# PSUM as four pairs of banks, scores evicted two heads at a time, key halves added for three units, in a new order

## The chip, the cores and the metric

The kernel runs on one core of one Trainium2 chip. Its metric is the device time of one execution in microseconds. Three runs of the kernel before gave 662.77, 663.51 and 665.59 us; their median is 663.51 us. The profile is one execution with its own time: its instructions span 661.4 us.

## The reference

One block of cross attention with an MLP, in float32. Batch 8, 256 queries and 256 keys, width 512, 16 heads of 32, inner width 2048. Cut to what matters:

```python
x1 = layer_norm(x) * ln1_w + ln1_b
q, k, v = x1 @ q_w + q_b, ctx @ k_w + k_b, ctx @ v_w + v_b      # 16 heads of 32
scores = einsum('bhqd,bhkd->bhqk', q, k) / sqrt(32)             # the mask is all ones
attn = softmax(scores)
out = einsum('bhqk,bhkd->bhqd', attn, v) @ cproj_w + cproj_b
hidden = out + x
y = layer_norm(hidden) * ln2_w + ln2_b
return hidden + gelu(y @ fc_w + fc_b) @ proj_w + proj_b
```

## The kernel before, in words

**Work.** The batch is done in two groups of four (g = 0, 1). The products with weights use two-by-two block schemes with seven products instead of eight (`quad`, line 857). A `quad` named, say, `o0_0` has products P1 to P7 on TensorE into three PSUM buffers X, Y and W, and evictions on DVE or ACT: `t1`, `t2`, `t3` and `c12` out of X after P1, P6, P5 and P3, `c11` out of Y after P2, `c22` and `c21` out of W after P7 and P4. X is written again by the next product only after its eviction. The sums of operands that the scheme needs (for example `a0t1` to `a0t4` of the attention output, `c0t` of the context, `z0i` in the last projection, `kws` of weights) run on DVE or POOL. The MLP (`fc`, `pd`) nests the scheme twice.

**Attention.** A unit `ghb` is group g, four heads (hg) and one batch element b; there are 32. Its steps are:
- `s` (line 1014): eight products of 32 rows on TensorE, four at a time, one head each, scores transposed (keys on partitions). Head j has a PSUM bank of 512 columns: 256 for each half of the 256 keys (kc).
- `ev` (line 1020, by the helper at line 618): ACT adds the mask's column and copies to SBUF, into `pr0` (heads 0, 1) and `pr1` (heads 2, 3). There are eight evictions of 128x256 in a unit, one for each head and key half.
- `mx`, `mt`, `mc`, `fold`: the maximum over keys, by DVE and small ACT copies; `md` and `mm` store it to DRAM and load it back spread over all partitions.
- `less` (line 1042, DVE or POOL) subtracts it, `exp` (line 1054, ACT) follows.
- `av` (line 1061): products with `ones`, which give the sum over the keys, and with v, which give the weighted values, both into one bank. For each head and each key half there is one of either, accumulated over the two halves.
- `r` and `att`: DVE inverts the sums and scales.

There is already a second form: where the letter of the unit in `KINDS` (line 494) is z, the two key halves are added first (`ss`, line 1057, DVE or POOL), and `ones` then takes four products instead of eight (line 1064). Before, all 32 letters are p, and that form is not used.

**Order.** `PROGRAM` (line 124) is one list of every step, written out: each engine's queue is the list's steps of that engine, in the list's order. A letter behind a colon says the engine where there is a choice (V DVE, A ACT, G POOL). All DMAs go on SP. `PLACES` (line 350) gives each buffer its slot. In SBUF the slots are numbered. In PSUM there are eight banks in two families, three W and five C: a scores unit takes any four C banks, and other buffers a bank of either family as `PLACES` says. The framework derives the waits: a buffer's first write waits until everyone is done with the slot's occupant before.

**Names of the prediction's steps.** `turn_c0_al` turns the context of group 0 (four transposes into a bank); `cq` loads it; `vw00` is a quarter of v's weight. `ab`, `a0t`, `o0_*`: bias, sums and output projection of group 0. `stats_y`, `eps`, `pow`, `nb`, `norm_y`, `turn_y`: the second normalisation and its turning. `less110_1` is the subtraction of the maximum in unit 110, heads 2 and 3.

Of the kernel before, what the change touches and what calls it, by code (L numbers as in the profile page):

```python
# [16 lines left out]
P = 128  # L17
# [6 lines left out]
BANKS = {"W": 3, "C": 5}  # L24
# [19 lines left out]
class Order:  # L44
# [49 lines left out]
    def run(self):  # L94
# [30 lines left out]
cq0_00_1 cq0_00_0 vw00 rows1 cq0_01_1 vw11 vw10 cq0_01_0 turn_c0_10 turn_c0_00 kw00 c0_10:V small cq0_11_0 c0_00:A  # L125
cq0_10_1 rows6 v0_0_P1 rows4 cq0_11_1 vws1:G fw0_00_1 turn_c0_11 fw0_11_1 turn_c0_01 vws2:G rows0 c0_11:V v0_1_P1
c0_01:A kw10 v0_0_t1:A fw0_11_0 c0t1:V fw0_00_0 fw0_10_0 v0_1_t1:A cq0_10_0 turn_c0_31 turn_c0_21 c0_31:V k0_1_P1
c0_21:A c0t2:V rows3 fw0i1_1:G k0_0_P1 fw0_10_1 fw0i4_1:G xt0_0 v0_0_P6 rows8 fw0i4_2:V fw0i4_3:G kws3:V vw01 xt0_7
fw0i4_4:G v0_1_P6 kw11 v0_0_t2:V xt0_6 fw0i1_2:V kw01 fw0i1_4:V c0t3:V v0_0_P5 v0_1_t2:A mk fw0s1:V xt0_2 turn_c0_20
vws4:G fw1_01_1 turn_c0_30 stats_x0_00:V c0_20:A xt0_1 v0_1_P5 c0_30:A fw0s3:V xt0_4 fw0i5_1:G v0_0_P2 v0_1_t3:V  # L130
v0_0_t3:A rows7 kws1:G fw0s2:V xt0_3 fw0_01_0 v0_0_P3 fw0i6_1:V rows2 fw0i7_3:G stats_x0_30:V k0_1_P7 fw1_00_1
v0_0_c12:A xt0_5 stats_x0_31:V stats_x0_01:A fw1_00_0 mk~1 fw0i7_1:V fw1_11_1 v0_1_P2 fw0i6_2:V rows5 fw0i6_4:V
fw0i1_3:V fcd0_7_False stats_x0_11:A fw0i6_3:V qw00 vws3:V v0_1_P3 fw1_10_1 eps_x0_0:V stats_x0_10:V fw1_10_0 pow_x0_0
fcd0_4_True nb_x0_0 eps_x0_1:G fw0i7_2:V k0_1_P2 v0_1_c12:A fw0i7_4:G qw10 fw1i1_3:V stats_x0_20:A kws2:G
stats_x0_21:V cols k0_0_P7 fw1_01_0 cols~1 fcd0_5_False pow_x0_1 fw0i5_3:V k0_1_t1:A fw1_11_0 fw0i5_2:V eps_x0_2:G
k0_0_t1:A eps_x0_3:G k0_0_P2 kws4:V norm_x0_01:A pow_x0_3 fw0_01_1 qw11 pow_x0_2 k0_0_P6 k0_0_c11 fcd0_1_True fw1s3:V
xt1_3 k0_1_P6 nb_x0_3 nb_x0_2 fw1i1_1:V norm_x0_21:A k0_0_t2:V fw1i1_2:G norm_x0_31:A nb_x0_1 k0_0_P5 norm_x0_00:V
fw0i5_4:G k0_1_t2:A v0_0_c11 norm_x0_11:A fcd0_5_True fw1i4_1:V fw1i1_4:V fcd0_7_True norm_x0_30:A k0_1_P5 k0_0_t3:V
fcd1_1_True fw1i4_2:G k0_1_c11 fcd0_6_False fw1s1:G fw1i4_4:V k0_0_P3 k0_1_t3:A xt1_2 norm_x0_10:A k0_0_c22 xt1_0
norm_x0_20:A k0_1_P3 v0_1_c11 k0_0_c12:A fw1i4_3:V c0t4:V turn_x0_00 k0_1_c22 turn_x0_10 x0_00:A turn_x0_11 fw0s4:V  # L140
qw01 qws1:G turn_x0_01 x0_10:A fcd0_6_True turn_x0_20 x0_01:A x0_11:V k0_0_P4 xt1_1 fw1i2_1:V fcd1_5_False fcd1_4_True
# [369 lines left out]
def tile_xattn_block(  # L511
# [154 lines left out]
    def col(i):  # L666
        return cols.t[:, i : i + 1]
# [838 lines left out]
```

## Time and profile before

| what | value |
|---|---|
| median of three runs | 663.51 us (662.77 to 665.59) |
| profiled execution: span of its instructions | 661.4 us |
| TensorE matmuls busy | 651.4 us (98%) |
| DVE busy | 571.6 us (86%) |
| ACT busy | 356.5 us (54%) |
| POOL busy | 450.4 us (68%) |
| DMA | 146.94 MB, mean 222 GB/s |
| granted TensorE clock | 1.00 |

The profiled execution's own time is that span; the runs' median lies 2.1 us above it, which holds what is around the first and last instruction and the scatter of runs. A float32 matmul stands as two records in the trace, so a `quad` product of two matmuls has four. Matmuls overlap: the mean of one record (about 380 ns for 256 columns) is longer than the step from one to the next, which the chain of waits shows. A "PE" row is a matmul, "PEld" a weight load. The idle time behind a row's bar is that of the engine ahead of the group's instructions, and the releaser is what ended most of it.

### The profile page before, as it was taken

The page shows a single profiled execution, that of the slowest core. Times are in us where ns is not written, and L with a number is a line of the kernel's source. Part 1 is how long each engine was busy: PE and PEld are TensorE (multiplying, and loading weights), DVE is VectorE, ACT ScalarE, POOL GpSimd, SP SyncE. Part 2 cuts the span into 40 slices and gives each one's busy share as a digit, 9 for nine tenths or more (in the row PEclk, how much of TensorE's full clock was granted, in tenths as well). Part 3 has the DMA queues.
Part 4 walks back from the last instruction along what each step waited for, and adds up shares of the span by engine and source line. Part 5 has one row for each costly group of instructions (what it writes and reads, how often), then busy time and mean ns, then how long its engine had stood idle before and what let it go on. Part 6 is the DMA issues. An engine that isn't in the chain of part 4 may idle for free.

```text
span 661.4 us, 11596 instructions
## 1 busy us (share of the span) xinstructions
PE 651.4 (98%) x3971; PEld 493.3 (75%) x3971; DVE 571.6 (86%) x935; ACT 356.5 (54%) x720; POOL 450.4 (68%) x397
## 2 busy tenths in 40 slices
PE   8999999999999999999999999999999999999997
PEld 6845464477545676787887878888888888888897
DVE  3989799879999999999989989987889779997573
ACT  2365698978989889837688890040222222730000
POOL 2476989868779996988999864659436046314882
PEclk9999999999999999999999999999999999999999
DMA  8999997889888568878555364979999995877256
GB/s 268 323 358 345 228 229 262 287 195 228 236 259 261 174 210 265 270 237 279 163 162 189 129 212 167 304 246 189 192 253 235 247 241 155 179 254 159 49 118 129
DMA packets 216538, 146.94 MB, mean 222 GB/s; under 512 B 125424, under 2 KB 176928, under 8 KB 216480
## 3 DMA queue, kind: packets, MB, share of 16 engines
q1 hardware_dynamic: 216480, 146.21, 78.9%
q8 instruction: 31, 0.51, 0.3%
q14 instruction: 27, 0.22, 0.1%
HBM read 105.67 MB, written 40.50 MB: 221 GB/s over the span
## 4 chain that ended last, share of the span: by engine, by line
PE 52%; DVE 5%; ACT 3%; DMA 1%; issue 1%; POOL 1%; SPq 0%; DVEq 0%
PE fc_X L638 14%; PE pd_X L638 14%; PE pd_W L638 7%; PE fc_W L638 6%; PE pd_Y L638 4%; PE fc_Y L638 3%; PE o_X L638 2%; DVE h L629 1%; PE av L638 1%; ACT pr L1054 1%; PE o_W L638 1%; ACT pr L618 1%; PE s L638 1%; DMA fl<-fcd 1%; DMA qw<-in_L_xattn_cproj_w_dram 1%
## 5 line engine op out<-in xcount | busy, mean ns | idle before, releaser
L618 ACT ACTIVATE pr<-s,cols 128x256 f32<-128x256 f32 x256 | 104.4, 483 | 17.4 <-PE s L638 10.6
L1051 POOL TENSOR_TENSOR pr<-pr,mm 128x512 f32<-128x512 f32 x72 | 98.4, 1393 | 7.7 <-DMA mm<-md 5.2
L1234 ACT ACTIVATE h<-h,cols 128x256 f32<-128x256 f32 x128 | 56.0, 499 | 55.7 <-DVE h L629 54.1
L1024 DVE TRANSPOSE_TENSOR_REDUCE mx<-pr 128x32 f32<-128x1024 f32 x64 | 77.5, 1222 | 2.5 <-ACT pr L618 2.4
L1054 ACT ACTIVATE pr<-pr 128x1024 f32<-128x1024 f32 x64 | 66.6, 1069 | 7.3 <-POOL pr L1051 4.1
L629 DVE TENSOR_TENSOR h<-fc_X,h 128x512 f32<-128x512 f32 x80 | 53.0, 679 | 7.1 <-PE fc_X L638 5.7
L1046 DVE TENSOR_TENSOR pr<-pr,mm 128x1024 f32<-128x1024 f32 x28 | 37.7, 1355 | 0.0
L629 DVE TENSOR_TENSOR h<-fc_W,h 128x512 f32<-128x512 f32 x48 | 32.1, 679 | 5.7 <-PE fc_W L638 5.5
L1033 ACT COPY mx<-mx 32x64 f32<-32x64 f32 x96 | 29.7, 309 | 11.9 <-DVE mx L1030 5.5
L638 PE MATMUL av<-pr,ones 128*32 128x256 f32 x512 | 34.1, 383 | 0.6 <-ACT pr L618 0.5
L610 ACT ACTIVATE e<-pd_X,cols 128x256 f32<-128x256 f32 x7 | 3.3, 471 | 57.0 <-PE pd_X L638 57.0
L629 POOL TENSOR_TENSOR h<-h,fl 128x512 f32<-128x512 f32 x9 | 12.3, 1368 | 25.7 <-DMA out_dram<-tq 22.4
L627 POOL TENSOR_TENSOR z1i<-z1t,z1i 128x512 f32<-128x512 f32 x8 | 10.0, 1270 | 25.5 <-DVE z1i L629 25.5
L638 PEld LDWEIGHTS av<-pr,ones 128*32 128x32 f32 x512 | 14.9, 109 | 16.1 <-issue 5.4
L638 PE MATMUL fc_W<-y1i,fl 128*128 128x256 f32 x100 | 24.5, 380 | 0.0
L638 PE MATMUL fc_X<-y1i,fl 128*128 128x256 f32 x88 | 22.5, 380 | 0.0
L638 PEld LDWEIGHTS fc_W<-y1i,fl 128*128 128x128 f32 x100 | 18.9, 190 | 2.9 <-DVE h L629 0.3
L605 ACT COPY h<-fc_X 128x512 f32<-128x512 f32 x16 | 9.1, 586 | 18.2 <-PE fc_X L638 14.2
L627 POOL TENSOR_TENSOR z1i<-h,z1i 128x512 f32<-128x512 f32 x10 | 13.4, 1362 | 7.8 <-ACT h L1234 4.1
L638 PE MATMUL pd_W<-z0i,pl 128*128 128x256 f32 x80 | 18.6, 379 | 0.0
L638 PEld LDWEIGHTS fc_X<-y1i,fl 128*128 128x128 f32 x88 | 16.7, 190 | 2.5 <-DVE h L629 0.3
L627 POOL TENSOR_TENSOR z0i<-h,z0i 128x512 f32<-128x512 f32 x10 | 16.3, 1653 | 1.4 <-DVE z0i L629 1.2
(601 smaller groups left out, 1905.6 us busy)
## 6 DMA issues: line engine op xcount, KB each, us to landing
mm<-md SPq DMA_DIRECT2D x32, 512.0 KB, 5.1
pl<-prd SPq DMA_DIRECT2D x54, 256.0 KB, 4.4
fl<-fcd SPq DMA_DIRECT2D x40, 256.0 KB, 4.5
fl<-prd SPq DMA_DIRECT2D x23, 256.0 KB, 4.6
fw<-in_L_xattn_fc_w_dram SPq DMA_DIRECT2D x16, 256.0 KB, 5.3
pw<-in_L_xattn_proj_w_dram SPq DMA_DIRECT2D x32, 128.0 KB, 4.2
hid<-in_x_dram SPq DMA_DIRECT2D x8, 512.0 KB, 7.8
hd<-hid SPq DMA_DIRECT2D x8, 512.0 KB, 3.9
```

The source lines that it names most:

```text
L605: (nc.scalar.copy if e == "ACT" else nc.vector.tensor_copy)(to(), of_())
L610: nc.scalar.activation(to(), of_(), AF.Identity, bias=bias(), scale=1.0)
L618: lambda e: nc.scalar.activation(to(), of_(), AF.Identity, bias=bias(), scale=1.0))
L627: nc.gpsimd.tensor_tensor(to()[:, ts(k, 512)], in0()[:, ts(k, 512)], in1()[:, ts(k, 512)], op)
L629: E[e].tensor_tensor(to(), in0(), in1(), op)
L638: nc.tensor.matmul(o(), l(), r(), start=first, stop=True, skip_group_check=True)
L1024: T.op(f"mx{u}_{h}", [("DVE", 1.126)], [(pr[h], None)], [(mx, [h])], lambda e, h=h: nc.vector.tensor_reduce(tile_of(mx)[:, 0:64].rearrange ...
L1033: lambda e, a=a: nc.scalar.copy(turned_()[0:32, 2 * a : 2 * a + 2, :], turned_()[32 * a : 32 * a + 32, 0:2, :]))
L1046: nc.vector.tensor_tensor(p_, p_, m_[:, :, None, :].to_broadcast([P, 2, 2, S]), ALU.subtract)
L1051: E[e].tensor_tensor(p_, p_, at(M, j)[:, None, :].to_broadcast([P, 2, S]), ALU.subtract)
L1054: lambda e, h=h: nc.scalar.activation(tile_of(pr[h]), tile_of(pr[h]), AF.Exp), table="exp")
L1234: lambda e, f=f, b=b, c=c: nc.scalar.activation(at(h[f][b], c), at(h[f][b], c), AF.Gelu_apprx_tanh, bias=col(c_fcb + f * 4 + c), scale=1.0 ...
```

## The change

Four edits in one:

1. PSUM is four tiles of two banks (B0 to B3). A scores unit takes two whole tiles, one for heads 0 and 1 and one for heads 2 and 3. Every other buffer takes half a tile, any of the eight.
2. A scores eviction reads one key half of two heads at once, 512 elements a partition in two runs of 256 out of two banks. A unit has four evictions instead of eight.
3. Three of the 32 units (012, 030 and 103) take the form with the key halves added first. Of their six additions two are on POOL and four on DVE.
4. `PROGRAM` and `PLACES` are new throughout: the order of each engine's queue, the choice of engine, the slots. The list was planned with delays drawn at random. The steps themselves are the same but for those of 2 and 3.

```diff
-BANKS = {"W": 3, "C": 5}
+BANKS = {"W": 8, "C": 8, "S": 4}
...
-                    w = where[b.name]
-                    b.home = w[0] if not w[0].isdigit() else b.kind
-                    b.slot = int(w.lstrip("WC"))
+                    b.slot = int(where[b.name])
...
-KINDS = ("pppppppppppppppp", "pppppppppppppppp")
+KINDS = ("pppppzzppppppppp", "ppppppppppzppppp")
...
-    halves = {}
+    halves, sides = {}, {}
...
+            elif b.kind == "S":
+                b.t = banks.tile([P, 1024], F32, tag=f"B{b.slot // 2}", name=b.name)
+                sides[b.slot // 2] = None
             else:
-                b.t = banks.tile([P, 512], F32, tag=f"{b.home}{b.slot}", name=b.name)
+                s, k = divmod(b.slot, 2)
+                if sides.get(s) is None:
+                    sides[s] = banks.tile([P, 1024], F32, tag=f"B{s}", name=b.name)
+                b.t = sides[s][:, ts(k, 512)]
...
-    first = banks.tile([P, 512], F32, tag="W0", name="first")
+    first = banks.tile([P, 1024], F32, tag="B0", name="first")
...
-        sb = [Buf(f"s{u}_{j}", "C", 2) for j in range(4)]
+        sb = [Buf(f"s{u}_{h}", "S", 4) for h in range(2)]
...
-            (lambda kc=kc, j=j: at(sb[j], kc), lambda kc=kc, j=j: row(k, j)[:, ts(kc, P)], lambda j=j: row(q, j), True)
+            (lambda kc=kc, j=j: at(sb[j // 2], 2 * (j % 2) + kc), lambda kc=kc, j=j: row(k, j)[:, ts(kc, P)], lambda j=j: row(q, j), True)
...
-            for j in range(4):
-                copy(f"ev{u}_{j}{kc}", (pr[j // 2], [2 * (j % 2) + kc]), (sb[j], [kc]), lambda j=j, kc=kc: at(pr[j // 2], 2 * (j % 2) + kc),
-                     lambda j=j, kc=kc: at(sb[j], kc), 256, lambda kc=kc: col(2 * (4 * g + b) + kc))
+            for h in range(2):
+                both = lambda t, kc=kc: t.rearrange("p (i k q) -> p k i q", i=2, k=2)[:, kc]
+                copy(f"ev{u}_{h}{kc}", (pr[h], [kc, 2 + kc]), (sb[h], [kc, 2 + kc]), lambda h=h, both=both: both(tile_of(pr[h])),
+                     lambda h=h, both=both: both(tile_of(sb[h])), 512, lambda kc=kc: col(2 * (4 * g + b) + kc))
```

Of the lists, the parts that the prediction speaks of, TensorE's steps alone. First the start, before and after:

```
before: turn_c0_10 turn_c0_00 small v0_0_P1 turn_c0_11 turn_c0_01 v0_1_P1 turn_c0_31 turn_c0_21 k0_1_P1 k0_0_P1
after:  small turn_c0_01 turn_c0_00 turn_c0_10 turn_c0_11 turn_c0_31 turn_c0_21 v0_1_P1 v0_0_P1 k0_0_P1
```

SP's first loads, before: cq0_00_1 cq0_00_0 vw00 rows1 cq0_01_1 vw11 vw10 cq0_01_0 kw00; after: cq0_00_0 cq0_01_0 cq0_01_1 cq0_00_1 cq0_11_0 cq0_11_1 vw00 vw11 vw10 vw01 kw00. Then the output projection of group 0 and what follows:

```
before: av033 o0_1_P2 o0_0_P2 s110 o0_0_P6 o0_1_P6 s130 o0_0_P5 o0_1_P5 s112 o0_0_P3 o0_0_P7 o0_1_P3 o0_1_P7
        o0_0_P4 o0_1_P4 s132 s101 av100 av110 av102 av122 av120 turn_y0_00
after:  av033 s110 o0_0_P1 o0_1_P1 s120 o0_1_P2 o0_0_P2 s130 o0_0_P6 o0_1_P6 s112 o0_1_P5 o0_0_P5 o0_1_P3 o0_1_P7
        o0_0_P3 o0_0_P7 o0_1_P4 s101 o0_0_P4 s132 av102 av100 av110 av122 turn_y0_00
```

DVE's queue after, around there: o0_0_c22 o0_0_c12 o0_1_c12 o0_1_c21 stats_y0_10 less110_1 o0_0_c21 stats_y0_00 stats_y0_11 stats_y0_20 aggr aggr aggr stats_y0_01 fold112 aggr aggr eps_y0_0 stats_y0_21 aggr nb_y0_1 nb_y0_0.

More of the change, by code (lines that the diff above doesn't have):

```diff
@@ L127 @@
[L127 to L141, printed above, removed]
@@ L212 @@
-ev112_30 o0_0_c22 exp122_0 o0_1_P7 mx112_1 exp102_1 pw1i4_3:G pw1_01_00 o0_0_c12 o0_0_P4 mm120 pw1i4_2:G pw1_10_00
-o0_1_c12 less110_0:G pw1_00_10 mt112 o0_1_c22 mc112_1 pw1_01_10 mc112_3 stats_y0_20 fl001_2 ev130_10 o0_1_P4 mc112_2
-mx130_1 exp102_0 less110_1:G exp122_1 o0_0_c21 s132 fold112 hd0 o0_1_c21 exp110_0 md112 hd3 stats_y0_21 s101 ev132_11
-pw1_00_00 pw1i4_4:G mx130_0 ev132_10 hd1 less120_1:G av100 ev101_00 fl001_0 exp110_1 stats_y0_11 pw1_01_01 stats_y0_01
-ev132_31 aggr_y0_20 ev101_01 aggr_y0_21 stats_y0_00 mm112 ev132_30 av110 stats_y0_10 ev101_31 eps_y0_2:G ev132_00
@@ L347 @@
-so1_12 pd14_P3 pd14_c22 pd14_P4 pd14_c12 st1 pd14_c21 st01
+cq0_00_0 cq0_01_0 cq0_01_1 cq0_00_1 cq0_11_0 cq0_11_1 vw00 vw11 vw10 small turn_c0_01 turn_c0_00 turn_c0_10 turn_c0_11
+turn_c0_31 turn_c0_21 c0_00:A c0_01:A c0_11:A c0_10:V c0t1:V c0_31:A c0_21:V c0t2:V v0_1_P1 v0_0_P1 v0_1_t1:A v0_0_t1:A
+vws1:G vw01 vws2:V vws4:G kw00 cq0_10_0 cq0_10_1 fw0_00_1 fw0_10_0 k0_0_P1 v0_0_P6 turn_c0_30 k0_1_P1 v0_0_t2:A v0_0_P5
+turn_c0_20 c0_20:A v0_1_P6 c0t3:V vws3:V mk fw0_11_1 fw0_11_0 fw0_10_1 fw0_00_0 rows1 rows4 fw1_11_1 kw01 xt0_1 kw10
@@ new lines @@
+xt0_5 rows6 rows2 fw0s1:V c0_30:V fw0s3:V fw0s2:V fw0i1_3:G fw0i4_1:G fw0i5_3:G kws3:G fw0i1_1:G fw0i1_2:G
+stats_x0_01:V v0_1_t2:V mk~1 fw0i7_1:V rows5 kw11 rows3 k0_0_P2 v0_1_P2 v0_0_P2 kws1:V kws2:V fw0i4_3:V v0_0_c11 c0t4:V
+xt0_6 xt0_7 rows8 rows7 rows0 xt0_4 fw0_01_1 xt0_0 fw0_01_0 fw1_10_0 xt0_2 xt0_3 fw1_01_0 fw1_10_1 cols v0_1_P5 cols~1
+v0_0_t3:A stats_x0_31:A stats_x0_30:A stats_x0_00:V eps_x0_3:V fw0i2_1:V k0_1_P2 stats_x0_21:A fw0i1_4:G fw0i5_1:G
+fw0i4_2:G fw0i4_4:G fw1_00_1 fw1_11_0 fcd0_4_True fw1_00_0 k0_1_P7 pow_x0_3 k0_0_t1:V fw0i7_2:G eps_x0_0:G fw0i6_1:G
@@ new lines @@
+mx110_0 mx110_1 mt110 mc102_2 ev120_00 mc110_2 ev120_01 mc102_3 a0t2:V o0_0_t1 fold100 mc110_3 mc102_1 mc110_1 a0t3:G
+a0t4:G ows4:G less122_0:G ows3:G o0_1_P2 o0_0_P2 s130 o0_0_P6 o0_1_t1 fold102 md102 fold110 md110 mm102 md100
+less102_1:G less122_1:V mx120_0 ev130_01 ev130_11 ev130_00 ev130_10 o0_1_P6 s112 o0_0_t2 o0_1_t2 mx120_1 mt120 mx130_0
+o0_1_P5 o0_1_t3 o0_0_P5 ev112_10 mc120_2 ev112_11 exp122_0 mx130_1 mt130 o0_0_t3 o0_0_c11 ev112_00 pw1_00_00 mm100
+pw1_11_10 less100_1:G mm110 fl001_0 pw1_10_11 pw1_00_10 pw1_11_11 less110_0:G less102_0:G o0_1_P3 o0_1_P7 less100_0:V
@@ new lines @@
+exp122_1 mc120_3 mc120_1 exp102_1 exp100_0 ev112_01 exp100_1 o0_1_c11 fold120 o0_1_c22 o0_0_P3 o0_0_P7 mx112_1 mx112_0
+mt112 o0_1_P4 o0_0_c22 o0_0_c12 o0_1_c12 o0_1_c21 stats_y0_10 s101 o0_0_P4 md120 pw1_00_11 mm120 fl001_2 pw1_10_01 hd1
+fl011_2 pw1_00_01 pw1_10_10 hd2 pw1_10_00 fl002_0 less110_1:V o0_0_c21 stats_y0_00 mc112_2 s132 stats_y0_11 stats_y0_20
+aggr_y0_10 aggr_y0_20 aggr_y0_11 stats_y0_01 mc112_1 mc130_3 mc112_3 exp110_0 fold112 aggr_y0_01 aggr_y0_00 ev101_00
+eps_y0_0:V exp102_0 mc130_2 ev101_01 exp110_1 less120_0:G ev132_01 ev132_10 ev132_00 ev132_11 mc130_1 ev101_11
@@ new lines @@
+eps_y0_1:G pow_y0_1 pow_y0_0 less120_1:G stats_y0_21 aggr_y0_21 nb_y0_1 nb_y0_0 av102 av100 av110 av122 norm_y0_00:A
+norm_y0_11:A ev101_10 norm_y0_01:A norm_y0_10:A exp120_0 turn_y0_00 stats_y0_31 mx132_0 y0_00:A exp120_1 turn_y0_10
+turn_y0_20 turn_y0_30 y0_10:A r102 stats_y0_30 fold130 mx132_1 att102 mt132 r122 aggr_y0_31 r100 fl001_3 fl011_1 hd3
+md112 pw1s3:G hd0 fl001_1 mm112 fc001_P1 fc011_P1 pw1i4_1:V eps_y0_2:V aggr_y0_30 y0_20:A mc132_2 fc001_t1:A mc132_1
+fc011_t1:A mc132_3 y0_30:A pw1s1:G y0i1_1:G eps_y0_3:G pow_y0_3 pow_y0_2 pw1i7_3:V y0i1_2:V av120 fc011_P6 fc011_P2
@@ L388 @@
-s100_0=W0 s100_1=W1 s100_2=4 s100_3=1 pr100_0=8 pr100_1=4 mx100=0 mm100=42 s120_0=4 s120_1=2 s120_2=1 s120_3=0
-pr120_0=18 pr120_1=66 mx120=0 mm120=76 s102_0=1 s102_1=4 s102_2=W1 s102_3=2 pr102_0=48 pr102_1=26 mx102=1 mm102=16
-s122_0=W0 s122_1=W1 s122_2=4 s122_3=2 pr122_0=74 pr122_1=2 mx122=2 mm122=14 av100=0 r100=3 rc100=2 att1_00=48 s110_0=0
-s110_1=W1 s110_2=1 s110_3=W2 pr110_0=72 pr110_1=82 mx110=2 mm110=38 av120=1 r120=12 rc120=6 att1_10=46 s130_0=2
-s130_1=0 s130_2=W1 s130_3=1 pr130_0=58 pr130_1=68 mx130=0 mm130=46 av102=3 r102=4 rc102=4 att1_01=88 s112_0=W2
@@ new lines @@
+ps_x0_00=3 x0_00=4 ps_x0_10=1 ps_x0_20=6 x0_10=66 ps_x0_30=2 ps_x0_01=0 x0_01=52 ps_x0_11=7 ps_x0_21=6 x0_11=46
+ps_x0_31=2 c0t1=38 c0t2=54 c0t3=22 c0t4=80 kw00=15 kw01=84 kw10=34 kw11=71 kws1=64 kws2=87 kws3=19 kws4=28 vw00=36
+vw01=63 vw10=8 vw11=72 vws1=37 vws2=45 vws3=20 vws4=29 qw00=21 qw01=44 qw10=46 qw11=85 qws1=12 qws2=52 qws3=42 qws4=65
+x0t1=40 x0t2=26 x0t3=74 x0t4=34 k0_0_X=3 k0_0_11=69 k0_0_Y=1 k0_0_21=68 k0_0_W=5 k0_0_22=76 k0_0_12=31 k0_1_X=6
+k0_1_11=2 k0_1_Y=2 k0_1_21=7 k0_1_W=4 k0_1_22=3 k0_1_12=1 v0_0_X=7 v0_0_11=62 v0_0_Y=2 v0_0_21=33 v0_0_W=5 v0_0_22=57
@@ new lines @@
+s100_1=4 pr100_0=50 pr100_1=18 mx100=1 mm100=78 s120_0=4 s120_1=6 pr120_0=4 pr120_1=6 mx120=2 mm120=78 s102_0=4
+s102_1=0 pr102_0=2 pr102_1=66 mx102=2 mm102=68 s122_0=4 s122_1=2 pr122_0=14 pr122_1=46 mx122=0 mm122=32 av100=2 r100=12
+rc100=9 att1_00=24 s110_0=6 s110_1=4 pr110_0=26 pr110_1=58 mx110=0 mm110=80 av120=4 r120=1 rc120=4 att1_10=46 s130_0=4
+s130_1=6 pr130_0=72 pr130_1=30 mx130=0 mm130=46 av102=3 r102=8 rc102=4 att1_01=26 s112_0=4 s112_1=6 pr112_0=74
+pr112_1=76 mx112=1 mm112=2 av122=1 r122=8 rc122=7 att1_11=78 s132_0=0 s132_1=6 pr132_0=68 pr132_1=84 mx132=2 mm132=8
@@ new lines @@
+av110=0 r110=11 rc110=6 s101_0=2 s101_1=4 pr101_0=48 pr101_1=32 mx101=2 mm101=16 av130=1 r130=6 rc130=4 s121_0=4
+s121_1=6 pr121_0=0 pr121_1=72 mx121=1 mm121=58 av112=3 r112=5 rc112=7 s103_0=6 s103_1=4 pr103_0=62 pr103_1=18 mx103=1
+mm103=68 ss103=66 av132=2 r132=7 rc132=4 s123_0=4 s123_1=6 pr123_0=16 pr123_1=30 mx123=0 mm123=66 av101=2 r101=7
+rc101=9 s111_0=6 s111_1=0 pr111_0=40 pr111_1=8 mx111=2 mm111=68 av121=4 r121=6 rc121=1 s131_0=2 s131_1=6 pr131_0=74
+pr131_1=68 mx131=2 mm131=82 av103=7 r103=2 rc103=9 s113_0=6 s113_1=2 pr113_0=12 pr113_1=66 mx113=0 mm113=80 av123=1
@@ new lines @@
+r123=8 rc123=4 s133_0=6 s133_1=0 pr133_0=40 pr133_1=16 mx133=1 mm133=20 av111=0 r111=4 rc111=2 av131=6 r131=4 rc131=1
+av113=1 r113=7 rc113=8 av133=7 r133=7 rc133=5 a0t1=80 a0t2=76 a0t3=48 a0t4=0 ow00=65 ow01=60 ow10=40 ow11=21 ows1=45
+ows2=11 ows3=56 ows4=88 hid0_0=8 hid0_1=16 hid0_2=22 hid0_3=82 o0_0_X=0 o0_0_Y=3 o0_0_W=7 o0_1_X=1 o0_1_Y=2 o0_1_W=6
+st_y0_0=2 mv_y0_0=7 rs_y0_0=5 xn_y0_00=1 xn_y0_01=19 st_y0_1=9 mv_y0_1=0 rs_y0_1=1 xn_y0_10=59 xn_y0_11=88 st_y0_2=8
+mv_y0_2=3 rs_y0_2=4 xn_y0_20=19 xn_y0_21=7 st_y0_3=6 mv_y0_3=8 rs_y0_3=9 xn_y0_30=12 xn_y0_31=42 ps_y0_00=6 y0_00=50
@@ L459 @@
+rl1=67 rq1_3=70 tq1_3=4 z1i4_1=54 z1i4_2=28 z1i4_3=76 z1i4_4=36 pl14_1=75 pl14_2=63 pl14_6=86 pl14_7=72 pl14_5=16
+pl14_3=53 pl14_4=33 pd14_X=1 ot0=80 pd14_Y=2 pd14_W=6 ot1=30
 """
```

572 lines of the change are left out of this document (267 added, 305 removed).

## The prediction

> **What bounds the kernel now.** I read the page first, then busy time by stage, then TensorE's waits, then the timeline where it waits longest.
>
> ```profile
> span 661.4 us, 11596 instructions
> PE 651.4 (98%) x3971; PEld 493.3 (75%) x3971; DVE 571.6 (86%) x935; ACT 356.5 (54%) x720; POOL 450.4 (68%) x397
> ```
>
> ```profile
> 0.00:20.00 20.00, 17.43 (x104) 13.96 (x105) 7.75 (x10) 4.12 (x6) 6.56 (x14) 1.00 0.88 281
> 180.00:260.00 80.00, 77.34 (x655) 49.58 (x655) 78.27 (x125) 72.31 (x150) 67.25 (x55) 1.00 0.76 239
> 100.00:180.00 80.00, 79.68 (x640) 48.00 (x632) 71.26 (x128) 69.64 (x147) 64.96 (x56) 1.00 0.87 242
> 260.00:380.00 120.00, 119.24 (x814) 93.97 (x813) 112.38 (x190) 91.69 (x181) 110.72 (x100) 1.00 0.63 202
> 380.00:660.00 280.00, 277.72 (x1404) 241.76 (x1402) 229.81 (x365) 67.02 (x131) 144.51 (x115) 1.00 0.80 197
> 640.00:661.40 21.40, 17.94 (x130) 16.91 (x128) 9.25 (x21) 0.00 (x0) 7.38 (x6) 0.98 0.63 120
> ```
>
> The columns are PE, PEld, DVE, ACT, POOL, then granted clock and DMA. TensorE is idle 10.0 us in all (661.4 less 651.4): 2.57 in the first 20 us, 3.46 in the last 21.4 us, and about 4 between. Of those, 0.32 lies in 100:180, 2.66 in 180:260, 0.76 in 260:380. The clock is full. So no order of the work can win much: **the ceiling on what a better order gives in the middle is about 4 us**, plus waits that hide as stretched matmuls. The stretch 180:260 is the one place where another engine is as full as TensorE: VectorE is busy 78.27 of 80 us, ScalarE 72.31.
>
> ```profile
> PE ps_c L725 <- DMA cq<-in_ctx_dram: 1.6, 2, 1.2
> PE o_X L638 <- DVE a0t L629: 1.0, 1, 1.0
> PE first L650 <- DVE warm L645: 1.0, 1, 1.0
> PE s L638 <- DVE q L629: 0.6, 1, 0.6
> PE av L638 <- ACT pr L618: 0.5, 2, 0.4
> PE fc_X L638 <- DVE h L629: 0.4, 2, 0.2
> ```
>
> ```profile
> 222.62 1.38 PE L638 MATMUL s<-vw,xt 32*128 32x256 f32 x16
> 222.75 2.25 DVE L629 TENSOR_TENSOR a0t<-att,a0t 128x1024 f32<-128x1024 f32 x1
> 225.05 2.21 PE L638 MATMUL o_X<-ows,a0t 128*128 128x256 f32 x9 [1.05 <-DVE a0t L629]
> ```
>
> The longest wait of the middle is 1.05 us at 225.05: the output projection waits for the token sum a0t.
>
> **The change part by part.** Prices come from the chain of waits, where TensorE's pieces stand end to end:
>
> ```profile
> 281.14 0.86 PE fc_Y L638 x4
> 285.45 1.86 PE av L638 x32
> 310.10 1.07 PE s L638 x16
> 412.84 1.73 PE pd_X L638 x8
> ```
>
> *Key halves added first (three units, 012, 030, 103).* A unit's av is 32 records in 1.86 us, 0.058 each. The product with ones is half of them, 16; with the halves added it needs 8. Saved: 8 x 0.058 = 0.465 us per unit, three units: **-1.40 us on TensorE**, which is the path. Added are six additions of 128x512, both operands in SBUF: two on POOL, four on DVE. The trace has no such addition of pr; the nearest rows are
>
> ```profile
> L1051 POOL TENSOR_TENSOR pr<-pr,mm 128x512 f32<-128x512 f32 x72 | 98.4, 1393 | 7.7 <-DMA mm<-md 5.2 <-issue 2.4
> L629 DVE TENSOR_TENSOR h<-fc_X,h 128x512 f32<-128x512 f32 x80 | 53.0, 679 | 7.1 <-PE fc_X L638 5.7 <-PE fc_W L638 0.5 <-DMA out_dram<-tq 0.2
> L629 DVE TENSOR_TENSOR h<-h,fl 128x512 f32<-128x512 f32 x5 | 5.3, 1058 | 0.1
> ```
>
> so 1.4 us on POOL and 0.68 to 1.06 on DVE; I take 1.06, the row whose operands also both lie in SBUF. They stand between exp and av. In the new order av stands 30.7 to 38.0 us of TensorE work after its scores in these units (counted with the prices above), which covers them: 0. Without cover, unit 030, whose two additions are both on POOL, would delay av by up to 2.8 us.
>
> *Evictions two heads at a time.* 256 ACTIVATEs of 128x256 become 128 of 128x512, each reading one key half out of two banks. The shape exists, out of one bank:
>
> ```profile
> L618 ACT ACTIVATE pr<-s,cols 128x256 f32<-128x256 f32 x256 | 104.4, 483 | 17.4 <-PE s L638 10.6 <-issue 2.9 <-PE av L638 1.2
> L610 ACT ACTIVATE xt<-q_X,cols 128x512 f32<-128x512 f32 x6 | 4.1, 691 | 2.7 <-PE q_X L638 2.7
> ```
>
> Before: 104.4 us, 0.408 each. After: 128 x 0.691 = 88.4, or 128 x 0.616 = 79 if they overlap as the small ones do (483 against 408). ScalarE loses 16 to 25 us. A read across two banks is in no row; its bounds are this and no saving at all (two small ones, 104.4). I take 16, for the shape is the row's. ScalarE is not the path (54% busy), so directly 0; in 180:260, at 90%, it shortens the queue of whatever TensorE waits for. That gain is in the order's term below.
>
> *PSUM as four pairs.* Before, a unit's scores took any four of five C banks, one by one; after, two whole pairs, and any product may use any bank. A pair is free only when both halves are. I counted TensorE work between the last product into a bank and the next occupant's first: under 1.3 us in 6 places before, in 2 after. One of the two is **zero**: o0_0_W is bank 7, scores 132 take banks 6 and 7, and o0_0_P4 stands directly ahead of s132 in the new order. So s132 must wait for the eviction o0_0_c21 on DVE, and DVE has o0_1_c21, a statistic (stats_y0_10) and less110_1 queued ahead of it:
>
> ```profile
> L1046 DVE TENSOR_TENSOR pr<-pr,mm 128x1024 f32<-128x1024 f32 x28 | 37.7, 1355 | 0.0
> L807 DVE BATCH_NORM_STATS2 st_y<-hid 128x6 f32<-128x512 f32 x16 | 10.5, 669 | 0.1
> L629 DVE TENSOR_TENSOR hid<-o_W,hid 128x512 f32<-128x512 f32 x8 | 5.4, 670 | 0.9 <-PE o_W L638 0.9
> ```
>
> From the end of o0_1_P4, DVE needs 0.67 + 0.67 + 1.36 + 0.67 = 3.4 us; TensorE has s101 and o0_0_P4 meanwhile, 1.07 + 1.73 = 2.8. If DVE comes without a backlog s132 waits 0.6 us for that and at least 0.67 for the eviction alone; with some backlog, more. I take **+1.3**, bounds 0.7 and 4 (a backlog of one more less and two evictions, 1.36 + 2 x 0.67). Behind s132 on TensorE stand av102, av100, av110, av122 and the turns of y0.
>
> *The new order.* All 612 DMA steps are there as before, on SP alone, in another order. 258 other steps change engine, nearly in balance (99 from POOL to DVE, 98 back, 61 between ACT and DVE); among them, net, four less from DVE to POOL (DVE -4 x 1.36, POOL +4 x 2 x 1.39). I count the places that gave waits.
> (a) Start. Before, the seventh 256 KB load is cq0_01_0; it lands at 10.1 us, and by then two turns and one product are done. A pair of turns takes 0.91 us (10.10 to 11.01), so that is 0.91 + 1.73 = 2.6 us. After, the seventh is vw00, and by then six turns can be done, 3 x 0.91 = 2.7.
>
> ```profile
> 4.65 1.41 PE L725 MATMUL ps_c<-ident,cq 128*128 128x128 f32 x8 [0.43 <-DMA cq<-in_ctx_dram]
> 10.10 1.07 PE L725 MATMUL ps_c<-ident,cq 128*128 128x128 f32 x8 [1.17 <-DMA cq<-in_ctx_dram]
> 11.01 1.89 PE L638 MATMUL v_X<-vw,c 128*128 128x256 f32 x8
> ```
>
> So 0, give or take one load's spacing, (10.10 - 4.65) / 5 = 1.1 us.
> (b) The wait at 225.05. Ahead of o0_0_P6, after the last av of batch group 0, stood two products and a scores: 2 x 1.73 + 1.07 = 4.5 us. After: four products and three scores, 4 x 1.73 + 3 x 1.07 = 10.1. The wait goes, and with it the stretched scores at 222.62 (1.38 against 1.07): **-1.35**.
> (c) The rest of 180:260, 2.66 - 1.05 = 1.6 us idle.
>
> ```profile
> L1077 DVE TRANSPOSE_TENSOR_REDUCE rc<-av 128x8 f32<-128x256 f32 x32 | 13.7, 429 | 2.5 <-PE av L638 2.4
> L1079 DVE RECIPROCAL rc<-rc 128x8 f32<-128x8 f32 x32 | 6.5, 203 | 1.1
> L1080 DVE STREAM_TRANSPOSE r<-rc 128x256 f32<-128x256 f32 x32 | 14.3, 445 | 1.2
> L629 DVE TENSOR_TENSOR att<-av,r 128x256 f32<-128x256 f32 x32 | 12.8, 407 | 0.3
> ```
>
> From the first maximum of group 1 (mx100) to the last bias of y0's first normalisation, the DVE queue holds 80 steps before and 71 after; three less (3 x 1.36), three inverses (0.43 + 0.20 + 0.45 each) and two scalings (0.41) left it, together 4.1 + 3.2 + 0.8 = 8 us of some 59 (each step at its row's mean). Where DVE is as full as TensorE this tells; I take -1.0, bounds -1.6 and +1 (they come later, in a stretch where DVE is 94% busy).
> (d) Elsewhere (0.32 + 0.76 us, and stretched matmuls): evictions with less than 1.3 us of other TensorE work before the next product into the same bank fall from 10 to 2. I take -0.6, bounds -1.1 and +0.5.
> (e) End: the last seven products of pd14 still end it, 0, bounds -0.5 and +1.
>
> Sum in the profiled execution's own time: -1.40 + 1.3 - 1.35 - 1.0 - 0.6 = **-3.05, so 661.4 becomes 658.3**. The median of the runs, 663.5, is 2.1 us above the span; what lies around the span does not change: **660.5**.
>
> **Rivals.**
> *B, all waits go.* The zero distance is covered, since DVE is emptier there by (c): -1.40 - 1.35 - 1.6 - 1.1 = -5.45, so 658.1; with hidden stretches of another 1 us, 657. For it: the distances are longer nearly everywhere. Against: c21 alone takes 0.67.
> *C, the change does not do what it says.* The waits only move: VectorE, not TensorE, sets 180:260, its total work stays within some 5 us of 571.6, and TensorE's saved 1.4 us is all that is left: 662.1. If the saved records too turn into waits for the six additions, 663.5.
> *D, slower: VectorE's queue between the output projection and the first MLP product.* s132 waits its upper bound 4 us. Then the normalisation of y0.
>
> ```profile
> L1034 DVE TENSOR_REDUCE mx<-mx 32x32 f32<-32x256 f32 x32 | 12.6, 397 | 3.2 <-ACT mx L1033 2.9
> L816 POOL TENSOR_TENSOR rs_y<-rs_y,neg_half 128x2 f32<-128x2 f32 x8 | 5.6, 699 | 3.2 <-DVE rs_y L813 2.8
> L827 ACT ACTIVATE v<-xt,rs_x 128x512 f32<-128x512 f32 x5 | 3.9, 804 | 0.0
> ```
>
> After o0_0_c21 stand five statistics, a fold (L1034) and some small steps, which I put at 0.6 in all (5 x 0.67 + 0.40 + 0.6 = 4.4), POOL's power 0.7, and four norms on ACT at 0.8 (3.2): 8.3 us, against s132 and four av, 1.07 + 4 x 1.86 = 8.5, ahead of the first turn; 11.6 us of other work stood there before. It decides from 0.2 us of extra delay on; with the fold and one less late, 2 us more. 4 + 2 instead of 1.3, and (c) at +1 instead of -1: 660.5 + 4.7 + 2 = 667.2. For it: 98% of DVE in that stretch, and a0t's one addition took 2.25 us where the L1046 row has 1.36 for the same size. Against: DVE has some 8 us less in the queue.
> A rule that speaks for D is in the Trainium skill, "SBUF — State Buffer", section Who interferes with whom: a DVE instruction with two SBUF inputs contends with a GpSimd instruction that reads SBUF. By that rule the four less moved to POOL would lengthen DVE's additions; the 2.25 us agrees with it, and D's price would be 0.9 more.
>
> **How the numbers follow.** What a measurement can tell from no change is 0.5%, 3.3 us: below 660.2, above 666.8. The forecast has 0.46, with its own range 658.5 to 662.5, two fifths of it under 660.2; B 0.17, C 0.21, D 0.16. Faster: 0.19 + 0.17 = 0.36; same: 0.27 + 0.21 = 0.48; slower: 0.16, since DVE's price can also come in part. The range reaches from B, 656.8, to D's middle, 667.0, and leaves out some 2 in 10.
>
> **What would show it.** TensorE's records fall by 24, av of three units to 1.4 us; ev in 128 pieces of 0.6 to 0.7 us, ACT about 335 us busy; no wait of o_X for a0t; a wait of s for hid (c21) near 230 us; PE idle in 180:260 near 1.6 instead of 2.66; the first 20 us within 1 us. Wrong it would be if DMA waits appeared in the MLP (none now), if the two-bank read took twice 0.4 us, or if the turns of y0 waited more than 2 us.

## The result, and the profile after

The changed kernel takes 834.6 us (median; 831.7 to 837.4) against 663.4 us before. The ratio is **1.258**, with a 95% interval of 1.254 to 1.261: slower by a quarter, 171 us, where 660.5 us and a range up to 667.0 were forecast. Nothing in the prediction comes near it, rival D neither.

The head of the page of the changed kernel, and the clock of its core:

```profile
span 835.6 us, 11385 instructions
PE 703.8 (84%) x3947; PEld 509.9 (61%) x3947; DVE 580.7 (69%) x942; ACT 337.5 (40%) x593; POOL 453.4 (54%) x396
PEclk9899999999999999999997999999999999989989
```

```profile
core 0: 835.6 us, clock 0.957
```

The work is what was predicted: 24 TensorE records less, ACT at 337.5 us. The time is not. TensorE is idle 835.6 - 703.8 = 131.8 us, where it was idle 10.0, and its matmuls count as busy for 52.4 us more (703.8 less 651.4), stretched by short waits and by a clock of 0.957 where it was 1.00. Together that is the 174.2 us between the spans. Of the other engines DVE grew by 9 us, to 580.7 of 835.6, and POOL by 3; ACT shrank. So no engine has become the bound.

Busy time by stage, columns as before (PE, PEld, DVE, ACT, POOL, clock, DMA), first after, then before:

```profile
0.00:20.00 20.00, 17.70 (x94) 15.03 (x95) 7.24 (x9) 4.61 (x7) 4.76 (x11) 1.00 0.88 277
180.00:260.00 80.00, 71.97 (x568) 41.42 (x568) 65.74 (x106) 60.72 (x101) 59.89 (x51) 0.98 0.74 197
420.00:460.00 40.00, 28.69 (x192) 19.54 (x196) 27.28 (x43) 20.23 (x36) 24.67 (x20) 0.84 0.21 68
700.00:740.00 40.00, 29.91 (x116) 24.20 (x116) 24.38 (x31) 17.11 (x42) 23.15 (x15) 0.88 0.37 89
```

```profile
420.00:460.00 40.00, 40.00 (x187) 35.24 (x186) 34.64 (x63) 8.73 (x18) 27.91 (x21) 1.00 0.87 242
500.00:540.00 40.00, 40.00 (x187) 35.03 (x186) 30.43 (x50) 10.41 (x22) 11.67 (x13) 1.00 0.98 238
```

The start is as before. From then on **TensorE and DVE are both less busy, in the MLP too**, where there are no scores, no evictions of scores and no added key halves: in 700:740 TensorE has 29.91 us of 40, and DVE, which it waits for, only 24.38. (ACT and POOL have some more in that stretch than in 500:540 before; over the whole span the share of every engine is lower.) Two engines that both wait: that is a matter of who waits for whom, not of work.

TensorE's waits in the changed kernel (what waits, for whom, us in total, times, longest):

```profile
PE fc_X L624 <- DVE h L615: 22.3, 14, 3.9
PE av L624 <- DVE h L615: 13.7, 6, 4.1
PE ps_c L624 <- ACT mv_x L788: 5.3, 1, 5.3
PE av L624 <- DVE z1t L615: 3.5, 1, 3.5
```

A name such as `av` is here that of the two-bank tile's first buffer; products of the MLP in the same tile carry it too. The longest `av` wait, in the timelines of TensorE and of DVE:

```profile
728.27 1.03 PE L624 MATMUL av<-y1i,fl 128*128 128x256 f32 x4
729.14 1.89 PE L624 MATMUL fc_X<-z1t,fl 128*128 128x256 f32 x8
735.15 2.07 PE L624 MATMUL av<-h,pl 128*128 128x256 f32 x4 [4.13 <-DVE h L615]
```

```profile
729.34 0.69 DVE L615 TENSOR_TENSOR h<-av,h 128x512 f32<-128x512 f32 x1 [0.17 <-PE av L624]
729.95 1.22 DVE L615 TENSOR_TENSOR z1t<-h,h 128x1024 f32<-128x1024 f32 x1
731.08 1.22 DVE L615 TENSOR_TENSOR z1i<-h,z1i 128x1024 f32<-128x1024 f32 x1
732.21 2.29 DVE L615 TENSOR_TENSOR z1i<-z1t,z1t 128x1024 f32<-128x1024 f32 x1
734.42 0.68 DVE L615 TENSOR_TENSOR h<-av,h 128x512 f32<-128x512 f32 x1
```

The product of 735.15 starts when DVE's addition of 734.42 ends. In the compiled program that product writes columns 512 to 767 of its tile, and the addition reads columns 0 to 511: **the other bank**. The product's own bank is free: its last reader was the addition of 729.34. DVE is late with that addition because three sums of 1024 stand ahead of it in its queue, which in the planned order did no harm, since nobody was to wait for it.

Counted over the compiled program, the kernel before has no wait between two engines that touch different banks; the changed one has 211: TensorE waits so for DVE 77 times and for ACT 12, DVE and ACT for TensorE 94 times, and DVE and ACT for each other 28. Theory T: the framework derives PSUM's waits by tile. Two banks in one tile are one thing to it, so a product into one half waits for the reader of the other half, and a reader for the product into the other. The 89 waits of TensorE would cost 171 / 89 = 1.9 us each. Such counts, here and below, depend on how a wait that covers several products is counted: another way of counting gives 85 for these 89, and 90, 195, 25 and 54 for the 110, 205, 23 and 49 further down. Without two-bank tiles it is zero both ways. So a cost per wait is rough.

### The profile page after: what moved, and what is told of

Its sections match the earlier page's. It is cut to its first block, busy times and chain, and to the rows that moved or that the text cites. A ratio compares the mean times of both kernels' runs of the same rounds, so it can differ in the third digit from the quotient of the medians.

```text
span 835.6 us, 11385 instructions
## 1 busy us (share of the span) xinstructions
PE 703.8 (84%) x3947; PEld 509.9 (61%) x3947; DVE 580.7 (69%) x942; ACT 337.5 (40%) x593; POOL 453.4 (54%) x396
## 5 line engine op out<-in xcount | busy, mean ns | idle before, releaser
L1038 POOL TENSOR_TENSOR pr<-pr,mm 128x512 f32<-128x512 f32 x80 | 111.4, 1418 | 41.4 <-DMA mm<-md 39.9
L604 ACT ACTIVATE pr<-s,cols 128x512 f32<-128x512 f32 x128 | 80.9, 686 | 54.6 <-PE s L624 42.7
L615 DVE TENSOR_TENSOR h<-av,h 128x512 f32<-128x512 f32 x49 | 33.0, 680 | 26.8 <-PE av L624 26.0
L615 POOL TENSOR_TENSOR tq<-tq,rq 128x512 f32<-128x512 f32 x10 | 15.4, 1549 | 25.4 <-DVE tq L1321 19.9
L613 POOL TENSOR_TENSOR z0i<-z0t,z0t 128x512 f32<-128x512 f32 x12 | 16.3, 1375 | 19.4 <-DVE a1t L615 8.4
L615 DVE TENSOR_TENSOR po<-fc_X,po 128x256 f32<-128x256 f32 x27 | 11.2, 418 | 18.6 <-PE fc_X L624 18.5
L615 DVE TENSOR_TENSOR h<-fc_W,h 128x512 f32<-128x512 f32 x23 | 15.6, 683 | 11.0 <-PE fc_W L624 7.0
L624 PE MATMUL fc_X<-z1i,pl 128*128 128x256 f32 x80 | 19.8, 399 | 0.0
L624 PEld LDWEIGHTS fc_X<-z1i,pl 128*128 128x128 f32 x80 | 16.5, 206 | 2.7
L1021 DVE TENSOR_REDUCE mx<-mx 32x32 f32<-32x256 f32 x32 | 12.4, 390 | 8.2 <-ACT mx L1020 8.2
```

The lines of the kernel that those rows point to most:

```text
L604: lambda e: nc.scalar.activation(to(), of_(), AF.Identity, bias=bias(), scale=1.0))
L613: nc.gpsimd.tensor_tensor(to()[:, ts(k, 512)], in0()[:, ts(k, 512)], in1()[:, ts(k, 512)], op)
L615: E[e].tensor_tensor(to(), in0(), in1(), op)
L624: nc.tensor.matmul(o(), l(), r(), start=first, stop=True, skip_group_check=True)
L1021: T.op(f"fold{u}", [("DVE", 0.25)], [(mx, [2, 3, 4, 5])], [(mx, [6])], lambda e: nc.vector.tensor_reduce(tile_of(mx)[0:32, 320:352], tile_ ...
L1038: E[e].tensor_tensor(p_, p_, at(M, j)[:, None, :].to_broadcast([P, 2, S]), ALU.subtract)
```

## The experiments

**One-bank tiles in the changed kernel.** The order, the places, the engines and the added halves stay. The lines for a scores buffer (`s` is `b.slot // 2`), then for any other:

```diff
             elif b.kind == "S":
-                b.t = banks.tile([P, 1024], F32, tag=f"B{b.slot // 2}", name=b.name)
...
+                    b.t = [banks.tile([P, 512], F32, tag=f"B{s}{k}", name=f"{b.name}{k}") for k in range(2)]
             else:
                 s, k = divmod(b.slot, 2)
...
-                b.t = sides[s][:, ts(k, 512)]
...
+                    b.t = banks.tile([P, 512], F32, tag=f"B{s}{k}", name=b.name)
```

> Edit: the changed kernel with eight PSUM tiles of one bank in place of four of two banks, in the same places; a score buffer is two such tiles, so each two-head eviction is again two of 128x256. The order, the engines and the three units with added key halves stay. Theory T (the framework keeps its waits by tile, so in a two-bank tile a product waits for the reader of the other bank, and the reader for the product): the loss goes, 657 to 664 us, TensorE idle under 12 us of the span. Rival R1 (the new order is at fault) and rival R3 (the additions of key halves are at fault): 800 us or more, since both are untouched. Rival R2 (reads across two banks, or two engines in neighbouring banks, are slow in the hardware): as T if it is the reads, 800 or more if it is the banks, which are the same.

Measured: 668.3 us, 1.0079 of before (1.0050 to 1.0109). The 166 us are gone; R1 and R3 fall as their cause, for the new order and the additions are all still there. R2 stays open here, since the reads across two banks are gone too. The time is some 4 us above T's range and slower than before, and TensorE is idle 671.8 - 655.4 = 16.4 us of the profiled span where under 12 was expected, which the last experiments take up.

**The other way round: the kernel before, only its tiles made two banks wide.**

```diff
-                b.t = banks.tile([P, 512], F32, tag=f"{b.home}{b.slot}", name=b.name)
+                s, k = divmod({'W0': 0, 'W1': 1, 'W2': 2, 'C0': 3, 'C1': 4, 'C2': 5, 'C3': 6, 'C4': 7}[f"{b.home}{b.slot}"], 2)
+                b.t = sides[s][:, ts(k, 512)]
...
+    for s in range(4):
+        sides[s] = banks.tile([P, 1024], F32, tag=f"B{s}", name=f"B{s}")
```

> Edit: the kernel before, with its own order, its 128x256 evictions and no added key halves, only its eight one-bank PSUM tiles declared as four of two banks (W0 with W1, W2 with C0, C1 with C2, C3 with C4). T: the changed kernel lost 171 us with 89 waits of TensorE for the other bank of a tile, 1.9 us each; here there are about 110 such waits, so 760 to 900 us. R1, R2 (reads across two banks) and R3: 660 to 667, since none of their causes is in it. R2 (engines in neighbouring banks): 663 too, the banks and their users are those of before.

Measured: 761.8 us, 1.1455 (1.1419 to 1.1490), at the low end of T's range. Only the declaration of the tiles is edited, so R1, R3 and the reads across two banks of R2 fall as the cause. The declaration also numbers the banks anew, one for one: a buffer keeps the sharers of its bank, but six of the eight lie elsewhere in PSUM. The control below has the same numbering. Its waits:

```profile
PE B L639 <- ACT pr L619: 21.1, 24, 2.4
PE B L639 <- DVE h L630: 7.7, 14, 1.4
```

`B` is the tile, `pr` the eviction of scores, now 24 times what TensorE waits for. Per wait for another bank (110) it is 98 / 110 = 0.9 us, half of what the changed kernel pays.

**Is it the width, or that a tile stays for many products?** In the changed kernel and in the last one a tile is kept, where before each buffer took its bank anew. The control keeps eight tiles of one bank; the dose goes up to two tiles of four.

Of the edit above only these figures differ (`{...}` stands for the same table of names):

```diff
-                s, k = divmod({...}[f"{b.home}{b.slot}"], 2)
-    for s in range(4):
-        sides[s] = banks.tile([P, 1024], F32, tag=f"B{s}", name=f"B{s}")
+                s, k = divmod({...}[f"{b.home}{b.slot}"], 1)                       # before_eight_tiles
+    for s in range(8):
+        sides[s] = banks.tile([P, 512], F32, tag=f"B{s}", name=f"B{s}")
+                s, k = divmod({...}[f"{b.home}{b.slot}"], 4)                       # before_in_fours
+    for s in range(2):
+        sides[s] = banks.tile([P, 2048], F32, tag=f"B{s}", name=f"B{s}")
```

> Edit: the control to before_in_pairs. The kernel before, its eight PSUM banks declared once as eight tiles of one bank that stay for the whole kernel, every product a part of one of them; before, each product declared its bank anew. In the changed kernel and in before_in_pairs a two-bank tile also stays for many products, so the loss could come from that and not from the width. T (the width: waits by tile): no wait for another bank is left, 661 to 667 us. Rival K (a tile that is kept for many products makes the waits coarse): as before_in_pairs, 740 us or more.

Measured: 663.0 us, 0.9984 (0.9966 to 1.0001); the same as before, down to the stage that was fullest:

```profile
180.00:260.00 80.00, 77.34 (x655) 49.57 (x656) 78.20 (x125) 72.33 (x150) 67.52 (x55) 1.00 0.76 238
```

Every product lies in the same physical bank here as in before_in_pairs and before_in_fours, with the same engines in the banks beside it. So R2's neighbouring banks are not the cause of those losses either.

> Edit: as before_in_pairs, but two tiles of four banks. T: three other banks to wait for in place of one, so clearly more than 761.8 us; TensorE has 209 waits for another bank here against 110 there, and at 0.9 us each, as there, that is 663 + 188 = 850; 820 to 950. Rival K: as before_in_pairs, 750 to 775, the tiles are kept as long.

Measured: 929.4 us, 1.3992 (1.3960 to 1.4024). Rival K falls twice: it is the width of the tile. A recount gives some 205 waits in place of the 209 of the expectation (four are inside one bank); 265 / 205 = 1.3 us each.

```profile
PE B L639 <- ACT pr L619: 62.2, 50, 4.4
PE B L639 <- DVE h L630: 40.1, 46, 1.8
```

**Doses in the new order.** `one_bank` with one, then two of the four pairs declared as tiles of two banks. `PAIRS` lists the pairs that are.

```diff
-PAIRS = ()
+PAIRS = (2,)         # one_pair
+PAIRS = (0, 1)       # two_pairs
```

> Edit: as one_bank, but the third of the four pairs is one tile of two banks. It is a dose: 23 waits of TensorE for the other bank instead of 89 in the changed kernel. T: 23 times 1.9 us, 44 us over one_bank, so 680 to 725 us, unless other waits cover them. R1 and R3: no different from one_bank.

> Edit: as one_bank, but the first and the second of the four pairs are tiles of two banks: 49 waits of TensorE for the other bank of a tile. One pair cost 44 us (712.2 less 668.3) with 23, all four 166 with 89. T: proportional, 49 times 1.9 us, so 745 to 775 us. If only one of the pairs mattered, 710 or less.

Measured: 712.2 us (1.0725, 1.0697 to 1.0752) and 738.5 us (1.1118, 1.1076 to 1.1160). One pair gives the 44 us foretold; two give 70, a little under the range. So the time rises with the number of pairs, but not in proportion to the count: 23, 49 and 89 waits cost 44, 70 and 166 us. In the wait of 735.15 the cost was how late the other bank's reader came; that this explains the uneven cost of the pairs was not measured.

**What is left: why 668 and not 660.** `one_bank` also undoes the wide evictions. They were put back without two-bank tiles, each reading one whole bank; and the same was done alone, in the kernel before. These kernels leave out that each key half goes to its own mask column and head, so they do the work but not the attention.

```diff
-                    for i in range(2):
-                        nc.scalar.activation(at(pr[h], 2 * i + kc), tile_of(sb[h])[i][:, ts(kc, 256)], AF.Identity, bias=col(2 * (4 * g + b) + kc), scale=1.0)
+                    to = tile_of(pr[h]).rearrange("p (i k q) -> p k i q", i=2, k=2)[:, kc]
+                    nc.scalar.activation(to, tile_of(sb[h])[kc].rearrange("p (i q) -> p i q", i=2), AF.Identity, bias=col(2 * (4 * g + b) + kc), scale=1.0)
```

> Edit: as one_bank, but a unit's scores are again evicted by four instructions of 128x512 instead of eight of 128x256. So that they stay in one-bank tiles, each reads one bank whole (the first key half's eviction the first head's bank, the second's the second's): it leaves out that each key half goes to its own mask column and head; the amount of work is that of the changed kernel. It asks why one_bank, at 668.3 us, is 7.8 us above the forecast of 660.5. Theory O (the new order itself has more waits than I priced, terms b to d): 665 to 670 us, as one_bank. Rival E (the order needs the lighter ScalarE; the narrow evictions of one_bank cost the difference): 657 to 662.

> Edit: the kernel before with the same eviction by four instructions of 128x512 a unit, each of one whole bank, each in the place of the earlier of the two that it replaces; it leaves out the same as one_bank_wide. It measures one part of the change alone. My term: ScalarE loses 16 to 25 us of 356 and the time stays, 662 to 665 us. Rival E: ScalarE sets part of the time between 180 and 260 us, 656 to 661.

Measured: one_bank_wide 665.5 us, 1.0026 (1.0006 to 1.0045); before_wide 662.6 us, 0.9996 (0.9977 to 1.0015). The first lies at the low end of O's range and above E's, so O holds, and E in part: the wide evictions are worth 1.0079 - 1.0026 = 0.53% (3.5 us, give or take 2.4) in the new order. In the old one no gain shows, though the scores' evictions take 23 us less there as well (all of ACT 18.6 us less, 337.9 for 356.5):

```profile
L631 ACT ACTIVATE pr<-s,cols 128x512 f32<-128x512 f32 x128 | 81.3, 686 | 24.7 <-PE s L651 17.7 <-issue 3.1 <-PE av L651 1.9
```

**The added key halves**, undone in one_bank and in one_bank_wide; the six `ss` steps leave `PROGRAM`.

```diff
-KINDS = ("pppppzzppppppppp", "ppppppppppzppppp")
+KINDS = ("pppppppppppppppp", "pppppppppppppppp")
```

> Edit: as one_bank, but units 012, 030 and 103 again take eight products with ones and their six additions are gone; the order is otherwise the same. It measures one term of the prediction, 1.40 us: T expects one_bank plus 1.4 us, 0.5 to 2.5. If the additions cost a wait, it is the same time as one_bank or faster.

> Edit: as one_bank_wide (the same part left out), but units 012, 030 and 103 take eight products with ones and have no additions. It measures the term of the key halves again, in the order with ScalarE's load as planned. My term: 1.4 us more than one_bank_wide. If the 4.5 us between one_bank_eight_ones and one_bank is the real size, 3 to 6 us more; if the additions cost what the products save, the same.

Measured: 1.0147 (1.0112 to 1.0182) against 1.0079, and 1.0101 (1.0076 to 1.0127) against 1.0026: the halves save 0.68% and 0.75%, 4.5 us (give or take 3.1) and 5.0 us (2.1). That is above the 0.5 to 2.5 of the first expectation and the larger size of the second, though the first interval still reaches down to 1.4. A part may be the clock: its mean over the runs is 0.999 with the halves and 0.998 without in the first pair, 0.998 and 0.995 in the second. Times the span that is 0.9 and 2.0 us, an estimate, and in the profiled run of one_bank_wide_eight_ones most of it lies in the first 20 us, ahead of any added half.

## Why the prediction was wrong, step by step

**The step that failed is "PSUM as four pairs", its term of +1.3 us.** It counted, for every bank, the TensorE work between a product and the next occupant *of that bank*, and found one place of zero distance. That place behaved: in one_bank_wide, s132 takes 1.98 us instead of 1.07, 0.9 us of wait for 1.3 foretold (bounds 0.7 and 4), and its second half waits for `hid`, which is c21.

```profile
245.37 1.99 PE L634 MATMUL o_W<-vws,a0t 128*128 128x256 f32 x8
247.30 1.98 PE L634 MATMUL s<-qws,q 32*128 32x256 f32 x16
```

```profile
248.15 0.72 PEld L634 LDWEIGHTS s<-qws,q 32*128 32x128 f32 x10 [0.55 <-DVE hid L625]
```

What the step did not ask is what the framework takes for one occupant. It said that a pair is free only when both halves are, and applied that to the scores alone, which fill a pair. Every other product shares its tile with a stranger in the other half, and in a two-bank tile the waits go by tile. That is 166 us (one_bank against the changed kernel), found in the old order too (98 us). With it the bounds "0.7 and 4", and so the range, were bounds of the wrong quantity. The distances should have been counted per tile, against DVE's and ACT's queues.

**The clock comes with the waits.** It falls to 0.84 in 420:460, where TensorE is busy 28.69 of 40 us, and its mean over the span is 0.99 to 1.00 in the kernels with one-bank tiles. In the changed kernel it is about half in the 5 us around the end of a wait of 3.9 us (at 441.6) and of the wait of 4.1 us (at 735.15):

```profile
440.00:445.00 5.00, 3.36 (x8) 2.73 (x9) 2.83 (x4) 2.85 (x5) 2.52 (x3) 0.54 0.01 3
735.00:740.00 5.00, 4.84 (x11) 3.87 (x12) 2.84 (x4) 0.00 (x0) 0.63 (x1) 0.50 0.00 0
```

Of the 174.2 us it can make at most (1 - 0.957) x 835.6 = 36, an estimate from the mean clock. The Trainium skill, "TensorE: Matmul & The Clock Gate", Part 1, says that the array's clock is halved after an idle window of about 3.4 us; the two places agree, and no wait of before, with 1.2 us at most, is that long. Long single waits are not the whole of it: in the first 20 us of one_bank_wide the clock is 0.91, and its longest wait there is 1.7 us.

**Evictions: right, with one condition.** 80.9 us for 128 were measured where 79 to 88 were given, and the read out of two banks costs no more than that out of one (686 ns, against 685 and 686 in the two wide kernels):

```profile
L604 ACT ACTIVATE pr<-s,cols 128x512 f32<-128x512 f32 x128 | 80.9, 686 | 54.6 <-PE s L624 42.7 <-POOL pr L1038 3.4 <-PE av L624 2.5
```

"0 on the path" holds for the old order (before_wide). In the new one, narrow evictions cost 3.5 us; by which wait is not shown.

**Key halves: the records are right, the size is not.** 24 records went, as foretold, and the additions cost about what was taken from the nearest rows (in one_bank_wide 0.68 to 1.15 us on DVE for 1.06, 1.28 on POOL for 1.4):

```profile
L625 DVE TENSOR_TENSOR ss<-pr x4: 679/782/1151, 128.4 to 341.4; 128x512 f32<-128x512 f32 x4
L625 POOL TENSOR_TENSOR ss<-pr x2: 1279/1280/1280, 129.3 to 138.1; 128x512 f32<-128x512 f32 x2
```

The saving is 4.5 to 5.0 us, not 1.4. The records explain 1.4 of it. What makes the rest, beside the clock, is not settled: one execution of each of the four kernels was profiled, and their runs scatter by 6 to 8 us. The prediction also misread where the additions stand: no unit has both on POOL (030 and 012 have one on DVE and one on POOL, 103 both on DVE). No term of its sum rests on that.

**The new order.** In one_bank_wide, where the false waits are gone, the steps can be read:

```profile
0.00:20.00 20.00, 17.17 (x99) 14.73 (x100) 8.36 (x9) 5.28 (x8) 4.38 (x11) 0.91 0.89 276
100.00:180.00 80.00, 78.37 (x596) 47.71 (x598) 71.46 (x121) 64.31 (x106) 65.77 (x55) 1.00 0.90 233
180.00:260.00 80.00, 79.31 (x662) 49.97 (x655) 76.68 (x131) 69.01 (x115) 71.04 (x56) 1.00 0.70 225
260.00:380.00 120.00, 119.46 (x833) 94.26 (x832) 115.54 (x197) 90.92 (x160) 106.66 (x98) 1.00 0.65 212
```

(a) The start is within 1.1 us, as said (idle 2.83 for 2.57; 2.30 in the changed kernel). (b) No product of the output projection waits for a0t any more. (b) and (c): 180:260 is idle 0.69 us where it was 2.66, a gain of 1.97 for the 1.05 + 1.0 = 2.05 given. (d) failed in 100:180: 1.63 us idle where it was 0.32 (260:380 gained 0.22). There I had not looked at the way of the maximum through DRAM. POOL waits for it 24.6 us, against 5.2 in the row of before:

```profile
L1049 POOL TENSOR_TENSOR pr<-pr,mm 128x512 f32<-128x512 f32 x80 | 107.7, 1371 | 24.7 <-DMA mm<-md 24.6
```

In some executions that reaches TensorE. In the profiled one of one_bank POOL, then ACT, then TensorE:

```profile
115.31 3.48 POOL L1049 TENSOR_TENSOR pr<-pr,mm 128x512 f32<-128x512 f32 x2 [3.03 <-DMA mm<-md]
...
118.82 1.06 ACT L1052 ACTIVATE pr<-pr 128x1024 f32<-128x1024 f32 x1 [3.56 <-POOL pr L1049]
...
121.91 1.93 PE L634 MATMUL av<-pr,ones 128*32 128x256 f32 x16 [2.87 <-ACT pr L1052]
```

The runs of one_bank_wide scatter from 661.9 to 669.5 us, and its profiled execution (span 661.1) is one of the short ones; how much of the scatter is this wait is not shown. So without the two-bank tiles, work and order as in the change take 1.0026 x 663.5 = 665.2 us, as far as one_bank_wide stands for them: inside the forecast's range, 4.7 us above its value, and no gain over before.

**The rivals.** None names the cause. B and C take the waits as they were; D had the right sign, but one place and 7 us, where the loss lies in every stage after the start.

## What to carry to other kernels

When a buffer is made part of a larger tile, ask what the framework tracks: count waits per tile, not per bank, and read the waits of the compiled program for pairs of instructions that share a tile but no bank. The sign in a profile is that TensorE and the engine that it waits for are both less busy than before in a stage whose work did not change. To read two banks at once without that price, by T, the tile has to belong to one user alone; whether four banks would then do for all the other buffers was not tried.

## What was not expected

That waits go by tile was not expected. For the same order and the same work, tiles no wider than one bank give 663.0 us, tiles of two banks 761.8 and of four banks 929.4. By the Trainium skill, "PSUM — Partial Sum Buffer", section Summary: rules for kernel authors, a reader beside a running matmul should be in another bank, with the waits set by bank. The chip agrees: with one-bank tiles, products and evictions in different banks run side by side at 663.0 us. What held the changed kernel was coarser than that rule.
